# A four-layer graph network on one core: layer 0's hyperedge gather in two fp32r parts, the degrees' count in one pass, and a second buffer for each one-hot

## The chip, the cores and the metric

The kernel runs on one core of a Trainium2 chip. A core has a matrix engine (TensorE, PE in the profile, with its weight loads as PEld), three engines for elementwise work (VectorE as DVE, ScalarE as ACT, GpSimd as POOL), a queue engine that issues most transfers (SyncE, SP), and 16 DMA engines. Times are microseconds on the device for one execution. The kernel before was timed in three runs: 1318.43 us in the median, 1313.73 to 1319.35.

## The reference

Eight graphs share 2048 nodes of 64 features (x is 8 x 2048 x 64) and one adjacency of 2048 x 2048, whose rows are divided by their sums. Four layers follow each other, each as `x = layernorm(x + layer(x))`:

- Layer 0: `A_stack = [I, A, 2 A A - I]`, `x_g = A_stack x`, and for each node its own weights, `w = embedding weight`, 64 x 64 for each of the three terms, from 16 embedding numbers.
- Layer 1: a hypergraph attention. With `h = x W`, scores `s = leaky_relu(h a_node)` and the incidence `H` (2048 nodes by 64 hyperedges), `alpha` is the softmax of s over the nodes of a hyperedge, and

```
agg = jnp.einsum('ben,bnf->bef', alpha, h)
```

  gathers the nodes' features into every hyperedge. Gates, a second softmax over the hyperedges of a node, an average over the neighbours (`adj / deg`) and a mix of two sources come after it.
- Layer 2: `x Ws + A x Wn + bias`.
- Layer 3: a graph convolution with `A + I`, normalised on both sides by `1 / sqrt(deg)`.

## The kernel before

**Precision.** Two number formats reach TensorE. A plain fp32 matmul is shown in the trace as two records; one on tiles that were rounded to fp32r (`r_()` in the code is that view of the same bytes) as one. Large products are done in fp32r without loss that matters: the adjacency becomes a mask of zeros and ones, [...] and the other side is written as a high part (rounded) and a low part (the rest), `hi + lo`, with one matmul for each into the same accumulator. The row's scale is applied to the sum.

**Tiling.** Nodes are cut into 16 tiles of 128. A tile's features for all eight graphs are 128 x 512. A product with the adjacency is 16 tiles times 16 tiles times two parts, 512 matmuls of 128x128 by 128x512.

**The first product** (`first_product`, L422) computes A x, in 32 pieces of the adjacency. Between the pieces, `memberships` (L304) prepares the lists of hyperedges of the nodes, a step at a time, in four quarters of 512 nodes: from the transposed incidence (pT) come running counts (pf, one matmul), and VectorE compares them with 1 and 2 (oh01, L379) and with 3 and the overflow's positions (oh23, L382 and L415). The results, one-hots, are stored to DRAM by SP (`store`, L337); layer 1 loads them again. VectorE also makes the masks m that TensorE multiplies by (L458).

**Layer 0** (`layer0`, L954) follows the order in which its loop is written (`program_order` ties each engine to it). Pass j treats tile j in eight turns g. In each turn, `weigh` (L1094) multiplies three terms (x, y1, y2) by one part of the weights into pp (12 fp32 matmuls, 24 records), and VectorE adds four slices of pp, each scaled by a column of the embedding, to the residual r (L1115). Between the turns stands other work, for neighbouring tiles:

- g = 0 to 2: the layernorm of tile j - 1, in three steps. sq (L1128, ScalarE) is its square, var (L1132, VectorE) the reader of sq. The result x1 goes to DRAM (kept, L1159). The first terms of tile j + 1 are prepared.
- g = 3: `project(j - 2)` (L1185): h and the neighbour features of tile j - 2, then md (GpSimd, L1197), which is the incidence of the tile twice side by side, and hs (GpSimd, L1219), which is h times the exponential of the score. After it, on TensorE, the 32 matmuls of the second product for tile j + 1 (y2p, L1067), then `to_features(j - 1)` (L1161: trx on TensorE, xT on ScalarE). On GpSimd, `scaled` (L1005): ms, and the sums cs of the mask over its column blocks.
- g = 5: `compare` (VectorE, L1022) tests the adjacency against the mask.
- g = 6: `second_term(j + 1)`, `scores(j - 1)` (sgp, es), and `gather(j - 2)` (L1223): one fp32 matmul, aggp += md x hs.
- g = 7: `degrees(j + 1)` (L1086): one fp32 matmul of cs with a column of ones, into dgp.

In pass 16 there is no tile left to weigh: the layernorm of tile 15 ends, tiles 14 and 15 are projected, `spread` (L1226) makes md for all tiles again, denominators are summed, the last two gathers are made, and matmuls of layer 1's first neighbour product (ind, L1252) are put between. Layer 1 begins with agg, aggp times the reciprocal of the denominators (L549).

**Buffers.** Tiles of layer 0 live in sixteen areas b0_0 to b0_15 of 128 x 512 that are free until layer 1; `homes` (L965) says which tag uses which: hs has area 5, sq has area 15, cs has 13 and 14. Tags without a home come from the pool l0s; x1 has one buffer. A write to a buffer waits until the readers of what lay there before are done. oh01 and oh23 have one buffer each, so a quarter's comparison waits for the stores of the quarter before.

Of the kernel before, what the change touches and what calls it, by code (L numbers as in the profile page):

```python
# [8 lines left out]
F32 = mybir.dt.float32  # L9
# [3 lines left out]
ALU = mybir.AluOpType  # L13
# [5 lines left out]
P = 128  # L19
NT = N // P  # L20
# [37 lines left out]
def r_(ap):  # L58
    return ap.bitcast(F32R)
# [3 lines left out]
def kernel(  # L63
# [33 lines left out]
    make_identity(nc, ident)  # L97
    ident_r = const.tile([P, P], F32, tag="ident_r", name="ident_r")
    nc.vector.tensor_copy(r_(ident_r), ident)
    ones = const.tile([P, P], F32, tag="ones", name="ones")  # L100
    nc.vector.memset(ones, 1.0)
    eps_t = const.tile([P, 1], F32, tag="eps", name="eps_t")
    nc.vector.memset(eps_t, EPS)
    flag = const.tile([P, 1], mybir.dt.int32, tag="flag", name="flag")
# [15 lines left out]
    def b_view(t2):  # L120
        return t2.rearrange("p (b c) -> p b c", b=B)

    def bcast(small):
        return small.unsqueeze(2).to_broadcast([P, B, C])
# [179 lines left out]
    def memberships(pre, ps, pm, fcw_sb, fcb_sb, fcg_sb):  # L304
# [59 lines left out]
        for q in range(NQ):  # L364

            raw = raws.pop(q)
            pT = pre.tile([P, QW], F32, tag="pT", name=f"pT_{q}")
            nc.vector.tensor_scalar(r_(pT), raw, 0.0, None, op0=ALU.is_gt)
            nc.sync.dma_start(lists["pT"][q], pT[0:E])
            yield  # L370
            pf = ps.tile([P, QW], F32, tag="li", name=f"pf_{q}")
            nc.tensor.matmul(
                pf, r_(tri.rearrange("p h e -> p (h e)")), r_(pT[0:E]), start=True, stop=True
            )
            yield
            pfm = raw
            nc.vector.tensor_tensor(pfm, pf, pT, ALU.mult)
            oh01 = pre.tile([P, QW], F32, tag="oh01", name=f"oh01_{q}")
            nc.vector.tensor_scalar(r_(oh01), pfm, order01, None, op0=ALU.is_equal)  # L379
            store(q, oh01, 0)  # L380
            oh23 = pre.tile([P, QW], F32, tag="oh23", name=f"oh23_{q}")
            nc.vector.tensor_scalar(r_(oh23[0:64]), pfm[0:64], 3.0, None, op0=ALU.is_equal)  # L382
            if q + 1 < NQ:
                load(q + 1)
            S = pre.tile([P, 4, P], F32, tag="S", name=f"S_{q}")
            yield
            for t in range(4):

                j = 4 * q + t
                cols = slice(t * P, (t + 1) * P)  # L390
                sm = ps.tile([P, QW], F32, tag="li", name=f"sm_{j}")
                nc.tensor.matmul(
                    sm[:, 0:E], r_(pT[0:E, cols]), r_(tri[:, 0, :]), start=True, stop=True
                )
# [559 lines left out]
    def layer0(  # L954
# [7 lines left out]
        raws, msk, terms, resid, norm, srow = {}, {}, {}, {}, {}, {}  # L962
        x1s, xTs, hps, hss, mds = {}, {}, {}, {}, {}

        homes = {"xT": (0, 1, 2), "xs": (3, 4), "hs": (5,), "y1T": (6, 7), "r": (8, 9),  # L965
                 "y2": (10,), "y2T": (11, 12), "cs": (13, 14), "sq": (15,)}
        turn = {}

# [36 lines left out]
        def scaled(j, h):  # L1005

            m = msk[j, h]
            ms = tile("ms", f"ms_{j}_{h}", (P, 8, P))
            nc.gpsimd.tensor_tensor(  # L1009
                ms, m, srow[j].unsqueeze(1).to_broadcast([P, 8, P]), ALU.mult  # L1010
            )
            cs = tile("cs", f"cs_{j}_{h}", (P, 4, P))
            nc.gpsimd.tensor_tensor(cs, m[:, 0:4], m[:, 4:8], ALU.add)
            nc.gpsimd.tensor_tensor(cs[:, 0:2], cs[:, 0:2], cs[:, 2:4], ALU.add)
            nc.gpsimd.tensor_tensor(cs[:, 0], cs[:, 0], cs[:, 1], ALU.add)
            if h == 1:
                nc.gpsimd.tensor_tensor(cs[:, 0], cs[:, 0], msk[j, 0, "s"][1][:, 0], ALU.add)
            msk[j, h, "s"] = ms, cs

        def compare(j, h):  # L1020
            ms, cs = msk[j, h, "s"]
# [64 lines left out]
        def degrees(j):  # L1086

            dp = ps_tr.tile([P, QW], F32, tag="tr", name=f"dgp_{j}")
            nc.tensor.matmul(
                dp[:, 0:1], msk[j, 1, "s"][1][:, 0], ones[:, 0:1], start=True, stop=True  # L1090
            )
            nc.scalar.copy(deg[:, j:j + 1], dp[:, 0:1])

# [91 lines left out]
        def project(j, h_first=False):  # L1185
# [8 lines left out]
                    )  # L1194
            if j not in mds:
                md = tile("md", f"md_{j}", (P, 2, E))
                nc.gpsimd.tensor_copy(md, pm[:, j, :].unsqueeze(1).to_broadcast([P, 2, E]))  # L1197
                mds[j] = md.rearrange("p h e -> p (h e)")

            def by_half(t):  # L1200
# [14 lines left out]
            if not stay:  # L1215
                for t, kept_part in zip((hi, lo), kept_i[j]):
                    nc.sync.dma_start(kept_part, t)
            hss[j] = tile("hs", f"hs_{j}", bufs=1)
            nc.gpsimd.tensor_tensor(  # L1219
                b_view(hss[j]), b_view(h_sb[:, j, :]), bcast(es[:, j, :]), ALU.mult  # L1220
            )

        def gather(j):  # L1223
            nc.tensor.matmul(aggp, mds[j], hss[j], start=j == 0, stop=j == NT - 1)  # L1224

        def spread():  # L1226

            mds.clear()
            for q, home in enumerate((1, 2, 3, 10)):
                md = own.tile([P, 4, 2, E], F32, tag=f"b0_{home}", name=f"md4_{q}")  # L1230
                nc.gpsimd.tensor_copy(
                    md, pm[:, 4 * q:4 * q + 4].unsqueeze(2).to_broadcast([P, 4, 2, E])
                )
                for t in range(4):
                    mds[4 * q + t] = md[:, t].rearrange("p h e -> p (h e)")
# [39 lines left out]
        def when(j, f, *args):  # L1275
            if 0 <= j < NT:
                f(j, *args)
# [8 lines left out]
        with program_order():  # L1286
# [6 lines left out]
            for j in range(NT + 1):  # L1293
# [4 lines left out]
                for g in range(8):  # L1298
# [37 lines left out]
                        when(j + 2, mask, 1)  # L1336
                    elif g == 5:
                        when(j + 1, compare, 1)
                        if j:
                            next(flags, None)  # L1340
                    elif g == 6:
# [808 lines left out]
```

## Time and profile before

| what | us |
|---|---|
| profiled execution | 1318.67 |
| its span, first to last instruction | 1316.8 |
| median of three runs | 1318.43 |
| TensorE busy | 1259.5 |
| VectorE busy | 885.0 |
| GpSimd busy | 483.5 |
| ScalarE busy | 368.4 |
| first product, in the chain of work | 6.9 to 150 |
| layer 0, first y2p to last pp | 155 to 700 |
| one pass of layer 0 | 34.0 |
| aggp, 16 fp32 matmuls: median of one record | 0.634 |
| dgp, 16 fp32 matmuls: median of one record | 0.260 |

The mean granted TensorE clock was 0.973. A record's duration is not what it adds to the time: matmuls are pipelined, so 32 of them with 0.39 to 0.5 us each follow each other in 7.5 us. What one adds is read from the distance between starts, or from the chain of work, which is the path followed back from the last instruction, at every step to what released it.

### The profile page before, as it was taken

To read this page: it belongs to the slowest core of one execution; us is meant where nothing else is said; L and a number is where in the kernel's file an instruction comes from. 1 tells how busy PE (TensorE), PEld (TensorE's weight loads), DVE (VectorE), ACT (ScalarE), POOL (GpSimd) and SP (SyncE) were. 2 spreads that over 40 slices of the span, in tenths; PEclk is the share of its full clock that TensorE was granted. 3 is DMA by queue.
4 is the path that set the end of the run, shared out by engine and by line. 5 is a ranking of instruction groups with operands and counts; after the bars stand their busy time and mean duration, and the time that the engine had idled before them with its cause. 6 is when DMAs were issued, how large, how long until landed. Compare 5 with 4: busy or idle time off the path is not lost.

```text
span 1316.8 us, 19976 instructions
## 1 busy us (share of the span) xinstructions
PE 1259.5 (96%) x7708; PEld 1002.4 (76%) x7708; DVE 885.0 (67%) x1595; ACT 368.4 (28%) x837; POOL 483.5 (37%) x403
## 2 busy tenths in 40 slices
PE   7999799999999999999999699999998899999996
PEld 6777588888888888888887467777776788888885
DVE  5555268888777877888664568878874655565544
ACT  3000001221122222221222356666664621111111
POOL 1000264444444444444411468888873600000000
PEclk9999799999999999999998589999998999999998
DMA  9887733332333332222272212222220133234551
GB/s 294 238 222 136 215 100 101 107 98 100 107 107 107 106 102 94 94 94 102 81 240 67 103 71 98 96 96 97 81 96 0 50 144 115 109 128 147 176 185 70
DMA packets 100791, 157.22 MB, mean 119 GB/s; under 512 B 12880, under 2 KB 64464, under 8 KB 94672
## 3 DMA queue, kind: packets, MB, share of 16 engines
q1 hardware_dynamic: 98208, 151.65, 35.7%
q10 hardware_dynamic: 2304, 4.20, 0.8%
q8 instruction: 63, 1.03, 0.3%
q0 software_dynamic: 176, 0.02, 0.1%
q14 instruction: 40, 0.33, 0.1%
HBM read 118.08 MB, written 37.76 MB: 118 GB/s over the span
## 4 chain that ended last, share of the span: by engine, by line
PE 89%; DVE 3%; DMA 2%; issue 2%; ACT 2%; POOL 1%; SPq 0%; ACTq 0%; DVEq 0%; POOLq 0%
PE pp L1104 25%; PE a L1418 18%; PE y2p L1067 9%; PE ind L1418 9%; PE y1p L490 8%; PE fc L805 3%; PE df L814 2%; PE gp L705 1%; PE yp L1508 1%; PE try L165 1%; PE trm L165 1%; PE aggp L1224 1%; PE hp L1192 1%; PE sgp L1171 1%; PE red L746 1%
## 5 line engine op out<-in xcount | busy, mean ns | idle before, releaser
L1115 DVE SCALAR_TENSOR_TENSOR r<-pp,emb_sb,r 128x256 f32<-128x256 f32 x512 | 247.4, 483 | 114.8 <-PE pp L1104 100.6
L1104 PE MATMUL pp<-w_sb,xT 64*128 64x256 f32 x1024 | 160.4, 390 | 1.7 <-DVE r L1115 1.7
L1104 PE MATMUL pp<-w_sb,y1T 64*128 64x256 f32 x1024 | 153.5, 376 | 0.0
L1104 PE MATMUL pp<-w_sb,y2T 64*128 64x256 f32 x1024 | 153.5, 376 | 0.0
L1053 POOL TENSOR_TENSOR r<-xs,bn 128x256 f32<-128x256 f32 x32 | 22.7, 731 | 277.2 <-issue 245.4
L1104 PEld LDWEIGHTS pp<-w_sb,xT 64*128 64x128 f32 x1024 | 94.4, 186 | 25.1 <-issue 14.9
L490 PE MATMUL y1p<-x_hi,m 128*128 128x512 f32 x256 | 106.2, 415 | 6.9 <-ACT x_hi L436 6.9
L1104 PEld LDWEIGHTS pp<-w_sb,y1T 64*128 64x128 f32 x1024 | 99.7, 187 | 10.9
L1104 PEld LDWEIGHTS pp<-w_sb,y2T 64*128 64x128 f32 x1024 | 99.6, 187 | 11.0
L1067 PE MATMUL y2p<-y_hi,msk 128*128 128x512 f32 x256 | 103.5, 404 | 0.0
L490 PE MATMUL y1p<-x_lo,m 128*128 128x512 f32 x256 | 103.0, 402 | 0.0
L1418 PE MATMUL ind<-y_hi,mj_l 128*128 128x512 f32 x240 | 101.7, 424 | 0.0
L1067 PE MATMUL y2p<-y_lo,msk 128*128 128x512 f32 x256 | 101.5, 397 | 0.0
L1418 PE MATMUL a<-v_hi,mj_l 128*128 128x512 f32 x256 | 100.1, 392 | 0.0
L1418 PE MATMUL a<-v_lo,mj_l 128*128 128x512 f32 x256 | 99.9, 391 | 0.0
L1418 PE MATMUL a<-y_lo,mj_l 128*128 128x512 f32 x240 | 95.1, 396 | 0.0
L1418 PE MATMUL a<-y_hi,mj_l 128*128 128x512 f32 x240 | 94.9, 396 | 0.0
L1418 PE MATMUL ind<-y_lo,mj_l 128*128 128x512 f32 x240 | 94.6, 394 | 0.0
L1009 POOL TENSOR_TENSOR ms<-msk,srow 128x1024 f32<-128x1024 f32 x32 | 89.8, 2807 | 5.3 <-DVE ms L1022 5.3
L737 POOL TENSOR_TENSOR ez<-ez,coef 128x1024 f32<-128x1024 f32 x32 | 69.8, 2182 | 56.3 <-DVE ez L735 54.3
L1001 DVE TENSOR_SCALAR msk<-adj 128x1024 fp32r<-128x1024 f32 x32 | 63.7, 2024 | 9.2 <-DMA adj<-in_at 9.2
L490 PEld LDWEIGHTS y1p<-x_hi,m 128*128 128x128 f32 x256 | 49.6, 194 | 19.0 <-ACT x_hi L436 6.9
(279 smaller groups left out, 2391.8 us busy)
## 6 DMA issues: line engine op xcount, KB each, us to landing
mj_l<-mask SPq DMA_DIRECT2D x46, 1024.0 KB, 4.9
raw<-in_at SPq DMA_DIRECT2D x32, 512.0 KB, 5.1
adj<-in_at SPq DMA_DIRECT2D x64, 256.0 KB, 3.8
mask<-msk SPq DMA_DIRECT2D x32, 512.0 KB, 4.6
xraw<-in_xn SPq DMA_DIRECT2D x8, 512.0 KB, 4.6
oh<-oh SPq DMA_DIRECT2D x32, 128.0 KB, 2.8
xT<-in_xt SPq DMA_DIRECT2D x16, 256.0 KB, 3.0
xs<-in_xn SPq DMA_DIRECT2D x16, 256.0 KB, 2.9
```

The lines of the kernel that those rows point to most:

```text
L165: nc.tensor.matmul(dst, src, ident, start=True, stop=True, is_transpose=True)
L490: nc.tensor.matmul(accs[q][jj], r_(m[:, t, jj * P:(jj + 1) * P]), r_(part[:, mt, :]), start=i + h + t == 0 and part is x_hi, stop=i == 3 a ...
L737: nc.gpsimd.tensor_tensor(by_b(ez), by_b(ez), per_b(coef, 2 * i, 2), ALU.mult)
L805: nc.tensor.matmul(fc[:, h, :], fcw_sb[rs], sT[rs], start=True, stop=True)
L814: nc.tensor.matmul(df[:, b:b + 1], th[:, b % 2, (b // 2) * P:(b // 2 + 1) * P], av_sb, start=True, stop=True,)
L1001: nc.vector.tensor_scalar(r_(m), raws[j][h], 0.0, None, op0=ALU.is_gt)
L1009: nc.gpsimd.tensor_tensor(ms, m, srow[j].unsqueeze(1).to_broadcast([P, 8, P]), ALU.mult)
L1053: nc.gpsimd.tensor_tensor(r[:, 4 * bq * C:4 * (bq + 1) * C] .rearrange("p (h l c) -> p h l c", h=2, l=2), swapped(terms[j]["xs"], bq), bn. ...
L1067: nc.tensor.matmul(acc, r_(msk[j, mt // 8][:, mt % 8, :]), r_(part[:, mt, :]), start=mt == 0 and part is y_hi, stop=mt == NT - 1 and part ...
L1104: nc.tensor.matmul(pp[:, h, pl, :], terms[j][name][rs, 2 * bq + pl], w_sb[rs, k, dq * 4 * C:(dq + 1) * 4 * C], start=k == 0, stop=k == K - 1,)
L1115: nc.vector.scalar_tensor_tensor(rb, ppv[:, :, dd, :], emb_sb[:, j, d:d + 1], rb, op0=ALU.mult, op1=ALU.add)
L1418: nc.tensor.matmul(acc, r_(a[:, mt, :]), r_(part[:, mt, :]), start=mt == 0 and part is hi, stop=mt == NT - 1 and part is lo,)
```

## The change

- `gather` for tiles 0 to 14 uses a high and a low part of hs, two fp32r matmuls in place of one fp32 matmul. Tile 15 keeps the fp32 matmul. hs itself is now written to area 15 (tag hsf), with sq; ScalarE copies it to the high part, in area 5; GpSimd subtracts to get the low part, in the buffer of x1, at g = 5 (`low_part`). md is written with the fp32r view.
- `degrees`: the last of the sums of cs is written, with the fp32r view, to a tile of its own (both, one buffer), and multiplied by two columns of ones in fp32r (ones_r, written once at the start).
- oh01 and oh23 have two buffers each.

The edits of `homes`, `md` and the declaration of ones_r are left to these words; the rest is:

```diff
-            oh01 = pre.tile([P, QW], F32, tag="oh01", name=f"oh01_{q}")
+            oh01 = pre.tile([P, QW], F32, tag="oh01", name=f"oh01_{q}", bufs=2)
...
-            oh23 = pre.tile([P, QW], F32, tag="oh23", name=f"oh23_{q}")
+            oh23 = pre.tile([P, QW], F32, tag="oh23", name=f"oh23_{q}", bufs=2)
...
+            msk[j, h, "s"] = ms, cs
             if h == 1:
-                nc.gpsimd.tensor_tensor(cs[:, 0], cs[:, 0], msk[j, 0, "s"][1][:, 0], ALU.add)
-            msk[j, h, "s"] = ms, cs
+                both = tile("both", f"both_{j}", (P, P), 1)
+                nc.gpsimd.tensor_tensor(r_(both), cs[:, 0], msk[j, 0, "s"][1][:, 0], ALU.add)
+                msk[j, "sum"] = both
...
             nc.tensor.matmul(
-                dp[:, 0:1], msk[j, 1, "s"][1][:, 0], ones[:, 0:1], start=True, stop=True
+                dp[:, 0:2], r_(msk[j, "sum"]), r_(ones_r), start=True, stop=True
             )
...
-            hss[j] = tile("hs", f"hs_{j}", bufs=1)
+            hs = tile("hsf", f"hs_{j}")
             nc.gpsimd.tensor_tensor(
-                b_view(hss[j]), b_view(h_sb[:, j, :]), bcast(es[:, j, :]), ALU.mult
+                b_view(hs), b_view(h_sb[:, j, :]), bcast(es[:, j, :]), ALU.mult
             )
+            if j == NT - 1:
+                hss[j] = hs,
+                return
+            hss[j] = tile("hs", f"hs_hi_{j}"), hs
+            nc.scalar.copy(r_(hss[j][0]), hs)
+
+        def low_part(j):
+            if j < NT - 1:
+                hi, hs = hss[j]
+                lo = tile("x1", f"hs_lo_{j}", bufs=1)
+                nc.gpsimd.tensor_tensor(r_(lo), hs, hi, ALU.subtract)
+                hss[j] = hi, lo
 
         def gather(j):
-            nc.tensor.matmul(aggp, mds[j], hss[j], start=j == 0, stop=j == NT - 1)
+            for part in hss[j]:
+                a, b = (mds[j], part) if j == NT - 1 else (r_(mds[j]), r_(part))
+                nc.tensor.matmul(
+                    aggp, a, b, start=j == 0 and part is hss[0][0], stop=j == NT - 1
+                )
...
                     elif g == 5:
                         when(j + 1, compare, 1)
+                        when(j - 2, low_part)
```

More of the change, by code (lines that the diff above doesn't have):

```diff
@@ L99 @@
     nc.vector.tensor_copy(r_(ident_r), ident)
+    ones_r = const.tile([P, 2], F32, tag="ones_r", name="ones_r")
     ones = const.tile([P, P], F32, tag="ones", name="ones")
     nc.vector.memset(ones, 1.0)
+    nc.vector.tensor_copy(r_(ones_r), ones[:, 0:2])
     eps_t = const.tile([P, 1], F32, tag="eps", name="eps_t")
@@ L963, in layer0 @@
         x1s, xTs, hps, hss, mds = {}, {}, {}, {}, {}
-        homes = {"xT": (0, 1, 2), "xs": (3, 4), "hs": (5,), "y1T": (6, 7), "r": (8, 9),
+        homes = {"xT": (0, 1, 2), "xs": (3, 4), "hs": (5,), "hsf": (15,), "y1T": (6, 7), "r": (8, 9),
                  "y2": (10,), "y2T": (11, 12), "cs": (13, 14), "sq": (15,)}
@@ L1196, in project @@
                 md = tile("md", f"md_{j}", (P, 2, E))
-                nc.gpsimd.tensor_copy(md, pm[:, j, :].unsqueeze(1).to_broadcast([P, 2, E]))
+                nc.gpsimd.tensor_copy(r_(md), pm[:, j, :].unsqueeze(1).to_broadcast([P, 2, E]))
                 mds[j] = md.rearrange("p h e -> p (h e)")
@@ L1231, in spread @@
                 nc.gpsimd.tensor_copy(
-                    md, pm[:, 4 * q:4 * q + 4].unsqueeze(2).to_broadcast([P, 4, 2, E])
+                    r_(md), pm[:, 4 * q:4 * q + 4].unsqueeze(2).to_broadcast([P, 4, 2, E])
                 )
```

## The prediction

> **What bounds the kernel now.** I read the page's busy times first, then a table of stretches, then the chain of work of one stage of layer 0, then TensorE's waits there, and last the two places where the change could touch the order of things: the end of layer 0 and the end of the first product.
>
> ```profile
> PE 1259.5 (96%) x7708; PEld 1002.4 (76%) x7708; DVE 885.0 (67%) x1595; ACT 368.4 (28%) x837; POOL 483.5 (37%) x403
> ```
>
> TensorE is busy 96% of the span. Matmul ends are modelled, so this alone proves little; the stretch from 500 to 600 us, which is the middle of layer 0, says more (columns: length, then busy time and instruction count of PE, PEld, DVE, ACT, POOL, then granted clock, DMA share, GB/s):
>
> ```profile
> core 0: us, PE busy (x) PEld busy (x) DVE busy (x) ACT busy (x) POOL busy (x), PEclk, DMA share, GB/s
> 500.00:600.00 100.00, 100.00 (x787) 83.74 (x787) 78.48 (x141) 20.09 (x40) 46.97 (x42) 1.00 0.32 106
> ```
>
> TensorE has no gap, at full clock; VectorE is at 78%, ScalarE at 20%, GpSimd at 47%, DMA at a third. The chain of work from 448 to 482 us, one stage of layer 0 (start, length, engine and tile), is TensorE alone:
>
> ```profile
> 447.94 7.53 PE y2p L1067 x32
> 455.47 0.44 PE trx L165 x4
> 455.91 7.97 PE pp L1104 x72
> 463.88 0.59 PE try L165 x4
> 464.47 0.79 PE sgp L1171 x8
> 465.26 0.96 PE aggp L1224 x2
> 466.22 2.79 PE pp L1104 x24
> 469.01 0.31 PE dgp L1089 x2
> 469.32 7.97 PE pp L1104 x72
> 477.29 0.58 PE try L165 x4
> 477.88 0.36 PE bp L1048 x2
> 478.24 2.79 PE pp L1104 x24
> ```
>
> The gather (aggp) holds 0.96 us of a stage of 34 us, in two records: one fp32 matmul is recorded as two. The degrees' count (dgp) holds 0.31, also two. The product y2p is fp32r already: 32 matmuls of the same shape, 128x128 by 128x512, in 7.53 us, 0.235 each. What TensorE waits for from 176 to 690 us (us in total, times, longest) is almost nothing:
>
> ```profile
> PE pp L1104 <- DVE r L1115: 1.7, 3, 1.1
> PE sgp L1171 <- DVE flagbox L281: 0.2, 1, 0.2
> ```
>
> So in layer 0 a microsecond less on TensorE is a microsecond less of time, until something else is late.
>
> [...] 0.96 against 0.235 us for the same shape is 4.1. [...] this trace has 1.27 us for 128x512 (cs at 459.77), and I use that.
>
> **The gather.** Removed: 15 of 16 fp32 matmuls (the last tile keeps its own). Added: 30 fp32r matmuls. At y2p's spacing a pair is 2 x 0.235 = 0.47, so a gather saves 0.96 - 0.47 = 0.49. Fourteen (tiles 0 to 13) lie in TensorE-bound time: 14 x 0.49 = 6.9 us. No trace shows fp32r between an fp32 sgp and an fp32 pp. If both weight loads came as bare as those of sgp, whose records follow each other at 0.1 us (0.79 for 8), the pair would be 0.47 + 2 x 0.1, and the saving 0.3 a gather, 4.2 us; if the switch to fp32 that L1224 shows start to start (1.03 us from 465.12 to 466.15) went too, 0.56 and 7.8 us. I take 6.9, since y2p follows fp32 hp and precedes fp32 trx without a gap.
>
> Added beside it, per tile: a ScalarE copy of hs to its high part, 128x512, 0.59 us (as L1166), and a GpSimd subtraction for the low part, 1.27 us as above. In the steady stage both are covered. hs ends on GpSimd at 450.2; ScalarE is then idle until y2 at 455.57. The low part stands in GpSimd's queue behind the mask sums, which end at 457.5, and needs the x1 buffer, which trx leaves at 455.9 and the store issued at 446.98 has left before. It ends near 458.8; the gather comes at 465.1. Cover: 6.3 us; beyond it every stage pays the excess. What stands behind the low part on GpSimd (ms, cs, y1, r) has the slack of r's idle time before it, 17 us. The new homes add waits that are over early: hs now shares a buffer with sq, whose last reader ends at 444.1, five us before hs; the next sq is written at 475.6, 17 us after the low part. SP issues the same transfers in the same order through all this. The copies of pm that round to fp32r are the same copies (0.30 us), and one sum of cs goes to a new tile: nothing.
>
> **The degrees' count.** Sixteen fp32 matmuls with one column become fp32r with two; one record in place of two. Half of 0.31 is 0.155, so 16 x 0.155 = 2.5 us saved. Not shown: such a matmul between fp32 ones. The ends are 0 (the switch is all of its cost) and 3.2 (0.2 each). I take 2.4, for a little overhead.
>
> **The end of layer 0.** Here no TensorE work covers latency. The timeline (start, length):
>
> ```profile
> 710.98 0.59 ACT L1211 ACTIVATE h<-hp 128x512 f32<-128x512 f32 x1
> 711.46 0.59 ACT L1166 COPY xT<-trx 128x512 f32<-128x512 f32 x1
> 711.65 1.04 POOL L1219 TENSOR_TENSOR hs<-h,es 128x512 f32<-128x512 f32 x1 [4.33 <-ACT h L1211]
> 712.11 1.05 PE L1171 MATMUL sgp<-wa,xT 128*128 128x4 f32 x8 [1.08 <-ACT xT L1166]
> 715.67 1.04 POOL L1219 TENSOR_TENSOR hs<-h,es 128x512 f32<-128x512 f32 x1 [2.97 <-PE aggp L1224]
> ```
>
> The copy of tile 14's high part is put into ScalarE's queue between h and xT of tile 15, and it waits for hs, which ends at 712.69. So xT of 15 starts at about 713.3 and not 711.46: sgp, es, hp, h of 15 and all behind them are 1.8 us later. Given back: today hs of 15 waits for gather 14 (one buffer; last line), and will not; and gather 14 is 0.5 shorter. Walking it through: gather 14 starts at 716.3, six early matmuls of 0.235 end near 718.2, hs of 15 is ready at 717.9, so the last gather starts at 718.0 to 718.2 where it was 716.77. Cost 1.3 us; bounds 0.5 and 1.9. The same copy at tile 13 delays xT of 14 from 686.9 to 688.8, but sgp wants it at 695.5: nothing. SP moves one mask load behind the last kept and xr transfers; the list loads behind it start at 719.1, after layer 0 frees its memory, anyway: nothing.
>
> **Two buffers for each one-hot.** They take away a wait of VectorE for the stores of the quarter before. In the trace of before there is one place where that can have bound:
>
> ```profile
> 122.90 1.02 DVE L379 TENSOR_SCALAR oh<-pT_raw,order 128x512 fp32r<-128x512 f32 x1
> 123.84 0.40 DVE L382 TENSOR_SCALAR oh<-pT_raw 64x512 fp32r<-64x512 f32 x1
> ```
>
> The other three L379 take 0.49, and this L382 follows 0.54 late. At most 0.5 us, in the last quarter; the end of the first product then hangs on a transfer of the one-hots (123.95, 11.6 us in the chain), on SP behind it, and on adj's masks. I take 0, bounds -0.5 and 0. One more VectorE copy of 128x2 at the start is 0.2 us (as the other small ones) while the first transfers are awaited: nothing.
>
> **The sum.** The profiled execution took 1318.67 us (span 1316.8), 0.2 above the median of 1318.43. 1318.67 - 6.9 - 2.4 + 1.3 + 0 = 1310.7; against the median 1310.4. I say 1310.5.
>
> **Rivals.** (a) *Half of it.* The fp32r pair pays its weight loads and the degrees gain nothing: -4.2 - 0.6 + 1.5 = -3.3, some 1315. For it: L1224 and dgp sit between fp32 matmuls of 64 rows, and "issue" gaps of 0.3 us stand at such switches on the weight loads' row. Against it: y2p has none. (b) *VectorE becomes the bound* behind the shorter stretch: near 1317. For it: pp waits for r now and then (1.7 us). Against: 78% busy and 76 us of waits for pp from 210 to 650. (c) *Slower:* GpSimd's writes rounded to fp32r (md 0.30, both 0.45, low part 1.27, 2.02 in all) are slow, since this trace times no such large operation. TensorE then waits at the gather for the low part. With a factor f the low part is 2.02 x (f - 1) later, the cover of 6.3 is used up at f = 4.1, and the change loses from f = 4.5 on; at f = 5 it is 1.8 us in 14 stages, 25 us, so about 1336. Against: DVE and ACT rows with fp32r outputs take what f32 ones take.
>
> **How the numbers follow.** Forecast 0.65, (a) 0.22, (b) 0.05, (c) 0.05; 0.03 is for a larger gain, near 1306. A measurement of this kernel can tell about 0.5%, 6.6 us; the runs before spread from 1313.7 to 1319.4. The gains' own bounds give 1318.67 - 7.8 - 3.2 - 0.5 + 0.5 = 1307.7 and 1318.67 - 4.2 - 0 + 1.9 = 1316.4; with the spread of runs below, 1305.5 to 1316. Below 1311.8 lies most of the forecast and the larger gain: faster 0.66; (a), (b) and the forecast's upper part: same 0.29; slower 0.05.
>
> **What would show it.** Right: aggp about 0.47 in the chain of a stage, dgp under 0.2, a stage of about 33.35 in place of 34, TensorE without waits for the low part, xT of tile 15 behind the high part's copy by 1.8 us, agg 1.2 to 1.4 us later in relation to the last trx. Wrong: a wait of aggp for GpSimd; a pair above 0.7; the first product ending earlier or later by over a microsecond, since the work there moves on transfers that I do not price.

## The result, and the profile after

The kernel after took 1314.09 us in the median of 20 runs (1310.22 to 1316.33), the kernel before 1317.99 beside it (20 runs, 1313.11 to 1322.38): a ratio of 0.9972, with an interval of 0.9959 to 0.9986. That is 3.9 us saved where about 8 were forecast. The time lies inside the range that was given, 1305.5 to 1316.

Two more comparisons of the same two kernels, on two chips, gave 0.9981 (0.9967 to 0.9995) and 0.9954 (0.9938 to 0.9970). The third lies outside the interval of the first: executions of one kernel differ by more than the interval from one set of runs says, and what they differ in is the granted clock of TensorE (the kernel before took 1312.34 us at 0.979 and 1322.97 at 0.970). Much of what follows is about telling that apart from the change.

First the page of the kernel after, its row of busy times, against 1259.5, 885.0, 368.4 and 483.5 us before:

```profile
PE 1253.7 (95%) x7692; PEld 1002.0 (76%) x7692; DVE 886.6 (67%) x1596; ACT 377.9 (29%) x852; POOL 514.4 (39%) x418
```

TensorE has 5.8 us less, GpSimd 31 more (the low parts), ScalarE 9.5 more (the high parts). The table of stretches from 500 to 600 us (columns as in the prediction) says that the steady stage has kept its bound:

```profile
500.00:600.00 100.00, 100.00 (x795) 84.37 (x791) 79.74 (x144) 22.53 (x44) 53.65 (x45) 1.00 0.31 106
```

TensorE is still without a gap, at full clock, and does 795 records where it did 787. The waits of TensorE from 176 to 690 us (total, times, longest) are what they were, and none is for GpSimd:

```profile
PE pp L1109 <- DVE r L1120: 1.8, 3, 1.1
```

So the low part is hidden, and VectorE has not become the bound. The distance from one y2 copy on ScalarE to the next, which is one pass of layer 0, fell from 33.99 to 33.48 us; 33.35 had been forecast. Where the 0.51 came from is read from TensorE's timeline in one pass (start, length; `64*128` are the rows and columns of the array in use), start to start. Before:

```profile
465.12 1.10 PE L1224 MATMUL aggp<-hs,md 128*128 128x512 f32 x2
466.15 0.70 PE L1104 MATMUL pp<-w_sb,xT 64*128 64x256 f32 x4
...
468.94 0.38 PE L1089 MATMUL dgp<-ones,cs 128*128 128x1 f32 x2
469.25 0.70 PE L1104 MATMUL pp<-w_sb,xT 64*128 64x256 f32 x4
```

After:

```profile
462.35 0.48 PE L1245 MATMUL aggp<-hs_hi,md 128*128 128x512 f32 x1
462.66 0.40 PE L1245 MATMUL aggp<-hs_lo,md 128*128 128x512 f32 x1
462.99 0.70 PE L1109 MATMUL pp<-w_sb,xT 64*128 64x256 f32 x4
...
465.78 0.27 PE L1094 MATMUL dgp<-ones_r,both 128*128 128x2 f32 x1
465.98 0.70 PE L1109 MATMUL pp<-w_sb,xT 64*128 64x256 f32 x4
```

The gather holds TensorE for 462.99 - 462.35 = 0.64 us where it held it for 466.15 - 465.12 = 1.03: it saves 0.39 to 0.40, not 0.49. The two matmuls come 0.31 and 0.33 apart, not 0.235. The degrees' count holds 0.20 where it held 0.31: it saves 0.11, not 0.155. Both together are the 0.51.

The rest of the shortfall is at the end of layer 0. The chain of work of the kernel after there (start, length, engine and tile; `issue` is time in which no wait shows):

```profile
705.08 1.05 POOL hs L1224
706.13 0.02 issue
706.15 0.02 ACT hs_hi L1231
706.17 0.50 issue
706.68 0.59 ACT xT L1171
707.26 0.04 issue
707.31 1.87 PE sgp L1176 x8
709.17 2.01 PE hp L1197 x16
711.18 0.52 PE denp L1262 x2
711.71 1.05 PE aggp L1245 x2
712.76 1.59 PE ind L1275 x6
714.35 0.86 PE aggp L1245 x2
```

The copy of tile 14's high part stands in front of xT of tile 15 and waits for hs. From trx of tile 15 to its sgp there were 1.74 us before (710.37 to 712.11); now there are 3.58 (703.73 to 707.31), 1.84 more, the very number that was forecast. But sgp then takes 1.87 us where it took 1.05, and hp 2.01 where it took 1.09: behind the hole TensorE works at half clock (a granted clock of 0.50 from 707.31 to 711.18). From the start of trx to the start of agg it is 11.52 us where it was 7.56, which is 3.96 more against the 1.3 of the forecast.

### The profile page after: what moved, and what is told of

It reads as the page before. It is cut to its first block, busy times and chain, and to the rows that moved or that the text cites. A ratio compares the mean times of both kernels' runs of the same rounds, so it can differ in the third digit from the quotient of the medians.

```text
span 1314.5 us, 19978 instructions
## 1 busy us (share of the span) xinstructions
PE 1253.7 (95%) x7692; PEld 1002.0 (76%) x7692; DVE 886.6 (67%) x1596; ACT 377.9 (29%) x852; POOL 514.4 (39%) x418
## 3 DMA queue, kind: packets, MB, share of 16 engines
q8 instruction: 63, 1.03, 0.3%
```

## The experiments

Two readings are used throughout. *Fourteen passes* is the time from the first y2 copy to the fifteenth; it is the same within 0.05 us in every profile of a kernel. Layer 0 is still filling in the first of these passes, so the fourteen hold 11 gathers and 14 counts of degrees. The *mean clock* is the granted clock of TensorE over a whole run, which every run lists. Within one kernel the time goes with it: of 56 runs of the kernel before on one chip, the 16 at 0.970 took 1322.07 in the median, the 16 at 0.973 took 1318.26, and the 10 at 0.978 took 1313.14. Over all runs of all kernels here, a thousandth of mean clock is 0.99 us, by the slope within the kernels. The last but one column of the table moves each kernel's mean to a clock of 0.973 with that slope (with twice its standard error), so that kernels can be compared whose runs happened to get different clocks. It also takes out a loss of clock that the kernel may itself have caused; that is why the medians stand beside it. It differs by 0.6 us between chips for the kernel before (1318.2 to 1318.8), and it is weakest for the kernel with the lowest clock, high part of 14 later, which it moves by 3.4 us.

| kernel | runs | median us | mean clock | mean us, moved to 0.973 | fourteen passes |
|---|---|---|---|---|---|
| before (all but the first comparison's) | 156 | 1318.21 | 0.9736 | 1318.5 ± 0.1 | 460.54 |
| after (all) | 53 | 1314.05 | 0.9716 | 1312.3 ± 0.3 | 454.66 |
| two buffers alone | 14 | 1320.28 | 0.9722 | 1318.8 ± 0.5 | 460.54 |
| degrees alone | 22 | 1316.82 | 0.9731 | 1316.1 ± 0.5 | 459.05 |
| gather alone | 11 | 1312.31 | 0.9736 | 1313.4 ± 0.5 | 456.08 |
| high part of 14 later | 9 | 1313.53 | 0.9696 | 1309.7 ± 0.8 | 454.64 |
| gather 14 in fp32 | 16 | 1311.62 | 0.9732 | 1311.6 ± 0.4 | 454.66 |
| hole filled | 16 | 1313.30 | 0.9708 | 1310.6 ± 0.4 | 454.66 |
| gathers beside y2p | 22 | 1313.32 | 0.9725 | 1313.1 ± 0.5 | 454.68 |
| all three moves | 14 | 1309.61 | 0.9727 | 1309.7 ± 0.4 | 452.5 |

**The parts one by one.** The two buffers alone, on the kernel before:

```diff
-            oh01 = pre.tile([P, QW], F32, tag="oh01", name=f"oh01_{q}")
+            oh01 = pre.tile([P, QW], F32, tag="oh01", name=f"oh01_{q}", bufs=2)
...
-            oh23 = pre.tile([P, QW], F32, tag="oh23", name=f"oh23_{q}")
+            oh23 = pre.tile([P, QW], F32, tag="oh23", name=f"oh23_{q}", bufs=2)
```

> The kernel before with two buffers for each one-hot and nothing else. Two readings are used for all runs: the length of a pass of layer 0 (distance of two copies of y2 on ScalarE, 33.99 us before, 33.48 after) and the end of layer 0, from the start of the last trx of layer 0 to the start of agg (7.56 us before, 11.52 after). Theory (the one-hots never waited for a store that mattered): pass 33.99, end 7.6, the first L379 of the last quarter still 1.02 us, time within 0.2% of before. Rival (the 0.5 us by which the first y2 came later after the change is the price of the buffers): the first y2 again 0.5 us later than 165.0, time 0.5 us longer.

Measured: 1.0009 (0.9995 to 1.0022), passes as before to the hundredth, and 7.55 us from trx to agg. The buffers give nothing. The slow comparison that the prediction had pointed to is still there in the kernel after; VectorE's timeline:

```profile
123.55 1.02 DVE L381 TENSOR_SCALAR oh<-pT_raw,order 128x512 fp32r<-128x512 f32 x1
```

It takes 1.02 us with two buffers as with one, so the store of the quarter before was not what it waited for. What slowed it is not shown; beside it GpSimd issues a transfer in each of these traces (L473, 1.17 us from 123.17 here).

The degrees alone (the declaration of ones_r, the sum in `scaled` and the matmul in `degrees`, as in the change):

```diff
-                dp[:, 0:1], msk[j, 1, "s"][1][:, 0], ones[:, 0:1], start=True, stop=True
+                dp[:, 0:2], r_(msk[j, "sum"]), r_(ones_r), start=True, stop=True
```

> The kernel before with the degrees' count in fp32r alone. Theory (a count goes from 0.31 to 0.20 us, not to half): pass 33.88, end of layer 0 7.6 us, time 1.7 us shorter. Rival (the halving that was forecast): pass 33.84 or less, 2.5 us shorter.

Measured: 0.9983 (0.9972 to 0.9994), a pass of 33.88: 0.11 saved. Fourteen passes save 1.49. From trx to agg it is 10.61, though, where 7.6 was expected: this kernel has 10.24 us of half clock at the end of layer 0.

The gather alone (homes, md, hs with its parts, `low_part`, `gather`, as in the change):

```diff
+            hss[j] = tile("hs", f"hs_hi_{j}"), hs
+            nc.scalar.copy(r_(hss[j][0]), hs)
...
+                nc.gpsimd.tensor_tensor(r_(lo), hs, hi, ALU.subtract)
...
+                a, b = (mds[j], part) if j == NT - 1 else (r_(mds[j]), r_(part))
```

> The kernel before with the gather's two parts alone. Theory (the pair takes 0.64 us start to start where fp32 took 1.03, and the end of layer 0 loses 4 us through the copy of the high part and the clock that falls while TensorE waits for it): pass 33.59, end 11.5 us, time 1.5 to 2 us shorter. Rival (the end lost its time to something in the other two edits): pass 33.59, end under 9 us, time 4 us or more shorter.

Measured: 0.9957 (0.9943 to 0.9971), a pass of 33.59: 0.40 saved. Fourteen passes save 4.46, which with the degrees' 1.49 is 5.95; the kernel after saves 5.88 (11 x 0.40 + 14 x 0.11 = 5.9). The parts add up. The wait for xT is there with the gather alone (3.58 from trx to sgp), and not with the degrees alone (1.74). To agg it is 11.51, as expected; but the time is 6.4 us below the kernel before on the same chip and not 1.5 to 2, and 5.1 at equal clock.

**The late xT.** The copy of tile 14's high part is moved behind xT of tile 15 on ScalarE:

```diff
-            nc.scalar.copy(r_(hss[j][0]), hs)
+            if j < NT - 2:
+                nc.scalar.copy(r_(hss[j][0]), hs)
...
             if j < NT - 1:
                 hi, hs = hss[j]
+                if j == NT - 2:
+                    nc.scalar.copy(r_(hi), hs)
```

> The kernel after, with the high part's copy of tile 14 moved behind the copy of xT of tile 15 on ScalarE, nothing else. Theory (that copy's place is the whole cause of the loss at the end of layer 0: 1.84 us by itself, 2 more by the clock in the hole it makes): last trx to agg 7.0 to 7.6 us, granted clock 1.0 in sgp, hp and gather, pass 33.48, time 4 us shorter than after and 6 to 7 shorter than before. Rival (the end loses to the shared areas or to GpSimd's low part): end 10 us or more.

Measured: 0.9961 (0.9946 to 0.9976), 5.2 us below the kernel before where 6 to 7 were expected. From trx to sgp it is 1.74 again, so the copy's place was the cause of the hole. But it is still 10.45 from trx to agg, and not 7.0 to 7.6. The timeline of this kernel there, its GpSimd line and the VectorE line beside it:

```profile
704.18 1.27 POOL L1241 TENSOR_TENSOR hs_lo<-hs,hs_hi 128x512 fp32r<-128x512 f32 x1 [0.73 <-ACT sg L1181]
704.20 1.27 DVE L1184 SCALAR_TENSOR_TENSOR es<-sg 128x8 f32<-128x8 f32 x1 [1.21 <-ACT sg L1181]
```

VectorE's es takes 0.17 us elsewhere (703.05 in the third profile of the kernel after); here it takes 1.27, started 0.02 after GpSimd's low part and ended 0.02 after it. That the one held up the other is read from these two lengths; no run tests it alone. So this move ended one wait, and es took 1.1 us more. Only 0.37 of it reach TensorE, in which denp waits for es (hp, at half clock, ends at 705.60). The rest of the 10.45 goes with half clock: 13.66 us of it stand between 693.86 and 710.93.

The kernel after once more, as a measure on the same chip as the next three:

> The kernel after once more, unchanged. Passes of 33.48 us and xT of tile 15 behind the high part's copy again, sgp 3.5 us after the last trx starts. Theory A (the fall of the clock to half at the end of layer 0 comes from the hole of 2.9 us before sgp, every time): sgp, hp and the gathers again at half clock, last trx to agg 11.5 us. Theory B (the clock is halved in blocks of 3.4 us whose place differs from execution to execution): the half-clock blocks lie elsewhere in relation to the last trx, and trx to agg is anything between 9.0 (full clock: 7.56 plus 1.84 less what the shorter gather and the second buffer give back) and 12 us.

Measured: 0.9981 (0.9967 to 0.9995), 1314.88. The profile is like the first: 3.58 from trx to sgp, sgp 1.87, 11.62 from trx to agg.

The gather of tile 14 in fp32 as before, without parts, so that nothing stands in front of xT:

```diff
-            if j == NT - 1:
+            if j >= NT - 2:
                 hss[j] = hs,
                 return
...
-            if j < NT - 1:
+            if j < NT - 2:
                 hi, hs = hss[j]
...
-                a, b = (mds[j], part) if j == NT - 1 else (r_(mds[j]), r_(part))
+                a, b = (mds[j], part) if j >= NT - 2 else (r_(mds[j]), r_(part))
```

> The kernel after, with the gather of tile 14 in fp32 as that of tile 15, so that no copy and no low part lie at the end of layer 0. Passes 33.48 us. Theory (the end loses 1.84 us by the late xT, and its hole makes half clock likelier): sgp 1.7 us after the last trx starts, time 2 to 4 us shorter than after again. Rival (the end is decided by the clock alone and the place of the copy hardly counts): within 1 us of after again.

Measured: 0.9950 (0.9931 to 0.9968), 1311.62, which is 3.3 below the kernel after on the same chip. From trx to sgp it is 1.74. Yet its profile also has 13.66 us of half clock and 10.65 from trx to agg, and of the 3.3 some 2.5 go with a better mean clock (0.9732 against 0.9708). What the hole itself costs is nearer to the 0.7 of the table than to the 3.3 of the medians: from the first y2 to agg, with 13.66 us of half clock in each, it is 548.8 here and 549.7 in the first profile of the kernel after.

**The switch.** Each gather is put behind hp and in front of y2p, which are already at such an edge (`gather(j - 3)` behind `project(j - 2)`):

```diff
                     elif g == 3:
                         when(j - 2, project)
+                        when(j - 3, gather)
...
                         when(j - 1, scores)
-                        if j < NT:
-                            when(j - 2, gather)
-                        else:
+                        if j == NT:
```

> The kernel after, with each gather one pass turn later, between hp and the 32 matmuls of y2p. Theory (a pair takes 0.64 us because its first matmul and the fp32 one behind it each come 0.1 us late at a change of format or of row group, as y2p's first does with 0.34): beside y2p it adds 0.46 and not 0.64, pass 33.30, 2.5 us shorter than after again. Rival (fp32r with these operands is slower by itself): the pair again 0.64 apart, pass 33.48.

Measured: 0.9971 (0.9958 to 0.9984), 1.6 us below the kernel after on the same chip where 2.5 were expected. TensorE's timeline in one pass:

```profile
474.83 1.06 PE L1197 MATMUL hp<-wb,xT 64*128 64x128 f32 x16
475.82 0.50 PE L1245 MATMUL aggp<-hs_hi,md 128*128 128x512 f32 x1
476.16 0.39 PE L1245 MATMUL aggp<-hs_lo,md 128*128 128x512 f32 x1
476.39 0.39 PE L1072 MATMUL y2p<-y_hi,msk 128*128 128x512 f32 x1
```

The first of a row of fp32r matmuls takes 0.34, every further one 0.23, and that first one comes once, whether it is aggp's or y2p's. A steady pass is 33.36, 0.12 less than after: 0.19 is saved at the gather, and 0.07 comes back at sgp, whose last matmul now stands in front of pp (the eight hold TensorE for 0.88, where it was 0.81). So the pair's surplus, some 0.1 us on each side of the gather, goes with its neighbours and not with its operands.

What stands at such an edge is seen in the weight loads (PEld). Before, at the start of a row of y2p, at its end, and at the gather:

```profile
447.87 0.19 PEld L1067 LDWEIGHTS y2p<-y_hi,msk 128*128 128x128 f32 x1
447.98 0.19 PEld L1067 LDWEIGHTS y2p<-y_lo,msk 128*128 128x128 f32 x1
448.21 0.19 PEld L1067 LDWEIGHTS y2p<-y_hi,msk 128*128 128x128 f32 x1
...
455.08 0.37 PEld L165 LDWEIGHTS trx<-ident,x 128*128 128x128 f32 x2
...
465.09 0.30 PEld L1224 LDWEIGHTS aggp<-hs,md 128*128 128x128 f32 x2
466.15 0.19 PEld L1104 LDWEIGHTS pp<-w_sb,xT 64*128 64x128 f32 x2 [0.76 <-issue]
```

After, at the gather:

```profile
462.32 0.19 PEld L1245 LDWEIGHTS aggp<-hs_hi,md 128*128 128x128 f32 x1
462.43 0.19 PEld L1245 LDWEIGHTS aggp<-hs_lo,md 128*128 128x128 f32 x1
462.99 0.19 PEld L1109 LDWEIGHTS pp<-w_sb,xT 64*128 64x128 f32 x2 [0.36 <-issue]
```

Within a row a load starts with the matmul in front of its own, 0.23 us early (448.21 for the matmul at 448.44). At an edge it starts with its own matmul (447.87; 462.99 and 466.15 for pp) or 0.03 early (462.32 for 462.35, 465.09 for 465.12). So the edges belong to both formats, and the fp32 gather paid them too: where its neighbours had 128 rows, in the kernel after at tile 15 (the last line of the chain above), it held TensorE for 0.86 us, and between sgp and pp for 1.03. The fp32 transposes trx (128 rows) follow the fp32r row without an edge, at 0.23 (455.08 to 455.31); pp (64 rows) does not. That the late load makes the edge is read from this order; no run tests it alone.

Over fourteen passes nothing of it is left (454.68 against 454.66): an early pass takes 34.24 where it took 33.56, and TensorE waits 2.8 us for VectorE's r where it waited 1.8; the rest of that loss is not found.

The three moves together: tile 14 in fp32, the gathers beside y2p, and the degrees' count at g = 6 ahead of the transposes of y:

```diff
                     elif g == 6:
+                        when(j + 1, degrees)
                         when(j + 1, second_term)
...
-                    elif g == 7:
-                        when(j + 1, degrees)
```

> e5_plain14 with the gather beside y2p and the degrees' count moved from behind the seventh to behind the sixth turn's weighing, ahead of the transposes try. Theory (the count pays 0.1 us for a change that it then shares with try): pass 33.20, and 5 us shorter than after again, 8 to 9 shorter than before. Rival: pass 33.30, since the count costs its 0.20 wherever it stands.

Measured: 0.9941 (0.9921 to 0.9962), 1310.92, which is 4.0 below the kernel after and 6.7 below the kernel before on the same chip, less than expected; but a steady pass of 33.09, less than either theory had. The count now stands between pp and the transposes, where an edge is paid anyway:

```profile
459.11 0.27 PE L1094 MATMUL dgp<-ones_r,both 128*128 128x2 f32 x1
459.24 0.66 PE L167 MATMUL try<-ident,y 128*128 128x128 f32 x4
```

It holds TensorE for 0.13 in place of 0.20, and the pp that it had cut in two, 2.79 and 7.97 us, take 10.56 in one piece. Together that is 0.27 a pass; the count's 0.20 had left out the edges in pp. The fifth to the eighth pass gain nothing. By its median this is the fastest version of all, ahead of both kernels.

**The clock.** Two theories for the half clock at the end of layer 0 were tested: A, that the hole in TensorE's work causes it; B, that it falls differently in every execution. Each kernel once more, for one profile:

> The kernel before once more, for a second profile of its end of layer 0. Theory A (a hole in TensorE's work is what halves the granted clock there, so that kernels without the late xT are spared): trx to agg 7.5 to 7.6 again, sgp of tile 15 at 1.05, full clock behind trx of tile 15. Theory B (where the clock is halved differs from one execution to the next, whatever the kernel): 7.5 to 10.7, and the half-clock stretches stand elsewhere than at 702.8 to 709.9; the span then goes with the mean clock of the execution, about 1.04 us for each 0.001: 1316.8 at 0.973, 1320 at 0.970, 1311 at 0.979. Both: 33.99 a pass.

> A third profile of the kernel before, with the same expectations as the second: A 7.5 to 7.6 from trx to agg again; B anything from 7.5 to 10.7, and a span that goes with the mean clock.

> A third profile of the kernel after. A: trx to agg 11.5 to 11.6 and sgp of tile 15 at 1.87, as in the first two. B: the wait for xT is 2.9 again, but the clock behind it may be full, and trx to agg then 9.2 to 9.5 (7.56 + 1.84, the six matmuls of ind not counted). Both: 33.48 a pass, 3.58 from trx to sgp.

Measured: the second profile of the kernel before has a span of 1312.5 at 0.978, no half clock at the end of layer 0 and 7.33 from trx to agg; the third has 1316.1 at 0.973 and 7.56. The third of the kernel after took 1309.35, with sgp at 1.05, 2.97 from trx to sgp (trx itself waits 0.53 for x here) and 9.84 to agg. The table of stretches, from 690 to 717 us, in the first profile of before, the second of before, the first of after and the third of after (the third number from the right is the granted clock):

```profile
690.00:717.00 27.00, 25.92 (x182) 21.41 (x179) 12.98 (x30) 5.45 (x13) 4.16 (x4) 0.87 0.10 30
```

```profile
690.00:717.00 27.00, 25.15 (x186) 19.98 (x182) 14.24 (x37) 6.29 (x14) 3.77 (x3) 1.00 0.15 42
```

```profile
690.00:717.00 27.00, 24.08 (x136) 19.75 (x135) 9.69 (x27) 6.47 (x15) 5.04 (x4) 0.75 0.11 36
```

```profile
690.00:717.00 27.00, 22.97 (x149) 17.55 (x146) 10.48 (x26) 6.77 (x13) 5.02 (x4) 0.94 0.32 103
```

The same kernel has 0.87 and 1.00, or 0.75 and 0.94. Read at finer steps, the stretches of half clock at the end of layer 0 are 3.41 or 6.83 us long in every profile, and longer elsewhere (27.31 us at 0.50, from 740.13 to 767.44, in the first profile of before): whole multiples of one length, but for the last, which ends with the kernel. Executions of one kernel have them at different places: between 690 and 717 us they start at 702.58 in the first profile of before, at 701.79 in the third and nowhere in the second; in the four of after at 696.03 and 706.27, at 695.26 and 705.50, at 703.63, and at 694.31 and 704.55. What sets the length and the starts was not shown. A as it was stated falls with the third profile of the kernel after, where sgp took 1.05 behind a hole; B stands for how much half clock an execution gets. The 3.58 from trx to sgp that both expected was missed, and so were B's 9.2 to 9.5 to agg. From trx to agg, though, the kernel before stayed at 7.33 to 7.56, as A had it: in its profiles half clock fell ahead of trx or not at all, and B's 10.7 was not seen. Whether a hole makes half clock likelier is a weaker claim. On the grid of 3.41 us that the starts and lengths in one profile make, half clock did follow that hole, one step later; the third profile of the kernel after:

```profile
700.22:703.63 3.41, 1.87 (x22) 1.85 (x24) 0.34 (x2) 1.51 (x5) 1.62 (x2) 1.00 0.12 44
703.63:707.04 3.41, 3.41 (x14) 2.71 (x11) 0.97 (x3) 1.12 (x3) 1.04 (x1) 0.50 0.00 0
```

In all eight profiles of kernels in which TensorE waits 2.2 to 2.9 us around this trx (the kernel after four times, the gather alone, the gathers beside y2p, and the two shifted ones below), the step that holds most of the wait is followed by half clock. Where it waits 1.1 to 1.4 us, that is so in six profiles of ten: not in the three of the kernel before and not with two buffers alone, but with the degrees alone, which has no late xT either. So a long wait was always followed by half clock here, and a short one often. Whether that makes the mean clock lower, the next kernel bears on. Six matmuls of ind, which until then stood behind gather 14, are put into the hole:

```diff
                         when(j - 1, to_features)
+                        if j == NT:
+                            early[0](3)
...
-            early[0](3)
             gather(NT - 1)
```

> The kernel after with six matmuls of layer 1's first neighbour product, which stood between the two last gathers, put behind trx of tile 15, so that TensorE works during 1.4 us of the wait for xT. trx to sgp stays 3.58 in both theories. A (the hole halves the clock): sgp of tile 15 takes 1.05 and not 1.87, trx to agg falls from 11.5 to 7.8 to 8.5 (1.4 moved, and some 2 of half clock gone), and the time is 2 to 3 below the kernel after, 1311 to 1312. B (the clock does not depend on it): trx to agg 10.1 (11.5 less the 1.4 moved) when halved, 8 when not, and the time 1.0 to 1.4 below the kernel after, near 1313.

Measured: 0.9965 (0.9948 to 0.9981), 1313.30; from trx to sgp it is 3.00, as in the third profile of after and not 3.58; TensorE waits 0.84 us for xT, sgp takes 1.05, but half clock runs from 703.22 to 710.05 and it is 11.11 to agg. Theory A's 7.8 to 8.5 is missed, and the mean clock over 16 runs, 0.9708, is no better than the kernel after's. B's 10.1 is missed too, by 1.0. At equal clock the time is 1.7 below the kernel after, near what B expects of the matmuls moved.

Last, kernels that only move the moment at which layer 0 ends. The count of tile 15 is made seven or fifteen times over:

```diff
-            nc.tensor.matmul(
-                dp[:, 0:2], r_(msk[j, "sum"]), r_(ones_r), start=True, stop=True
-            )
+            for _ in range(15 if j == NT - 1 else 1):
+                nc.tensor.matmul(
+                    dp[:, 0:2], r_(msk[j, "sum"]), r_(ones_r), start=True, stop=True
+                )
```

> The kernel after again, as the measure for the two shifted ones: 1314.0 to 1314.9 in the median, mean clock over its runs 0.9705 to 0.972.

> The kernel after with the degrees' count of tile 15 made seven times over (the same result each time), which moves the end of layer 0 by six times 0.13, some 0.8 us, and nothing else. Theory H (the hole lowers the clock, wherever it falls): mean clock as in the kernel after, within 0.0007, and 0.8 us more. Theory P (the clock is set window by window, some 3.4 us each, and what counts is where the sparse stretches fall in the windows): the mean clock over the runs moves by 0.001 or more, up or down, and the time by 1 us or more against the 0.8 that was added.

> The same with fifteen counts in place of one, a shift of fourteen times 0.13, some 1.8 us, about half of a stretch of half clock. H: mean clock as in the kernel after, and 1.8 us more. P: the mean clock moves by 0.001 or more; if the windows run from the program's start, this shift should show the most, up to 0.003, and the time could then even be below the kernel after.

> The fastest version again (tile 14's gather in fp32, the other gathers beside y2p, the counts ahead of the transposes of y), for more runs: 1309.5 to 1311.5 in the median, ratio to before 0.993 to 0.996.

Measured: the kernel after 1311.78 (0.9954), mean clock 0.9728; six counts more 1313.51 (0.9961, 0.9949 to 0.9973), 0.9725; fourteen more 1312.04 (0.9950, 0.9931 to 0.9969), 0.9738; the three moves 1308.61 (0.9927, 0.9893 to 0.9960), 0.9740. In the profile of the larger shift the counts hold TensorE for 1.76 us (665.81 to 667.57) where one holds it for 0.20. The kernel after missed its own expectation by 2 us and more, at a better clock than in its other comparisons, and the three moves theirs by 0.9, downwards too. Against this kernel after, the small shift leaves the clock alone, as H expects, and the large one lifts it by 0.0010, the least that P asks; their times move by 1.7 and 0.3 us where H has 0.8 and 1.8. With 20 and 10 runs beside 10 of the kernel after, and 0.9708, 0.9718 and 0.9728 for one and the same kernel in three comparisons, this decides nothing between H and P. That the clock is set in windows was the author's supposition; the traces show the lengths, 3.41 us and its multiples.

## Why the prediction was wrong, by its steps

**What bounds the kernel, and what is hidden: right.** TensorE kept its 100% in the steady stage; no wait for the low part came up; VectorE at 79.7% is no bound. Rivals (b) and (c) did not come. (The rows with fp32r outputs that spoke against (c), in the trace of before, for 128x512: ScalarE 0.60 us for y_hi in fp32r and 0.59 for h in f32, both from hp; VectorE 0.68 for y_lo in fp32r at L880 and 0.68 for y2T in f32.) GpSimd's low part, written rounded to fp32r, took 1.27 us (704.18 above), as estimated.

**The gather: of the terms in the sum, the one that failed most.** "I take 6.9, since y2p follows fp32 hp and precedes fp32 trx without a gap." The second half is so, but trx has 128 rows and pp, which stands behind the gather, 64: the one follows the last fp32r matmul at 0.23, the other at 0.33. The first half was a misreading: 0.235 is 7.53 us divided by 32, and the mean hides the first of the row, which comes 0.34 apart (447.87 to 448.21 in the profile before, then 448.44). A row of 32 pays the edge once, a pair pays it once too, on 2 matmuls. So 0.47 was the price of a pair without edges, which takes 0.64 in its place; and the 0.96 set against it, read from the chain, was short of the 1.03 that the fp32 gather held TensorE start to start. Measured, a gather saves 1.03 - 0.64, some 0.40, where 0.49 was taken: 14 x 0.40 = 5.6 and not 6.9. It lies between the two ends that the prediction had named, 0.3 and 0.56; it had priced each of the two corrections, and took neither.

**The degrees: right in kind, too large.** 0.11 each and not 0.155: 16 x 0.11 = 1.8 and not 2.4. Two records became one, but the count still holds TensorE for 0.20, not for 0.155. "For a little overhead" had taken off 0.1 in all, where 0.7 was due.

**The two buffers: right.** Nothing, and the slow L379 did not wait for a store.

**The end of layer 0: the wait right, its cost right only at equal clock.** Where half clock lay ahead of trx, sgp came 1.84 us later, for the reason given and to the hundredth (in the chain above ScalarE begins hs_hi at 706.15 and xT behind it at 706.68; that it would keep this order was the author's estimate); with full clock there (the second profile of before, the third of after) it was 1.5 later, 2.97 behind trx and not 1.50. The first profile shows 3.96 us, not 1.3. To compare at an equal share of half clock, take the executions that have about 6.83 us of it between 690 and 717: before, twice, 552.94 us from the first y2 to agg; after, in its fourth profile, 547.07. That is 5.9 saved. With 3.41 us of it, the two buffers alone have 551.37 and the kernel after, in its third profile, 545.45: 5.9 again. The passes give 5.6 + 1.8 = 7.4, and so the end costs about 1.5, near the forecast.

**What the sum left out: the clock.** With the sizes measured the sum is -5.6 - 1.8 + 1.5 = -5.9, and the column at equal clock says 1312.33 - 1318.46 = -6.1 (on the two chips by themselves -6.3 and -6.4). The medians differ by 4.2, in the first comparison by 3.9; the mean clock was 0.9716 against 0.9736, and 2.0 thousandths are 2.0 us. So of the 4.1 us between the forecast's 8.0 and the 3.9, the gather accounts for 1.3, the degrees for 0.6, the end for 0.2, and the clock, a term that the sum put at nothing, for about 2. The prediction worked with one profile, in which the clock behind trx of tile 15 was full, and read the spread of the runs as noise without asking what it was made of.

Whether the change costs clock, or these runs had less of it, stays open. For it: over the pooled runs the difference is several times its standard error (0.0002 and 0.0003); half clock at the end of layer 0 was 13.65, 13.65, 3.41 and 6.82 us in the four profiles of after, and 6.83, none and 6.83 in the three of before (elsewhere in the run 63 to 64, and 60 to 67); and it followed the late xT every time. Against the hole as its cause: the kernel with gather 14 in fp32 has no hole and 13.66, the one with the degrees alone none and 10.24; the one with the hole filled has the mean clock of the kernel after; the gather alone has the hole and 0.9736. And against any firm answer: the same kernel got 0.9708 in one comparison and 0.9728 in another, beside 0.9742 and 0.9732 for the kernel before.

Rival (a), "half of it", forecast -3.3 and is near in number; its mechanism is half true. The edges are real and cost 0.1 us each. But it had put the degrees' gain at 0.6, and it did not have the clock, which is about half of what is missing in the medians.

## What to carry to other kernels

Price a short burst of matmuls from the first record of a row, start to start, not from the mean of a long row, and what it replaces in the same way; and put a small matmul where an edge is paid anyway (the degrees' count, moved so, gained 2.1 us over fourteen passes). Before a change of half a per cent is judged, lay the times of the runs beside their granted clocks: here one kernel spread over 10 us with its clock, and intervals from the runs of one comparison were too narrow. When an operation is moved off a queue, ask who will run beside it in its new place: with the high part moved out of xT's way, VectorE's es took 1.27 us beside GpSimd's low part, 1.1 more than elsewhere, of which 0.37 reached TensorE.

## What had not been expected of the hardware

- The granted clock at the end of layer 0 falls to half in stretches of 3.41 or 6.83 us, which start elsewhere in each execution (in the three profiles of the kernel before at 702.58, nowhere, and at 701.79). A wait of 2.2 to 2.9 us of TensorE there was followed by one in eight profiles of eight. With the mean clock, runs of the kernel before went from 1312.34 to 1322.97 us (156 runs, correlation -0.96).
- An edge between two kinds of matmul cost about 0.1 us, in fp32 and in fp32r: 0.31 to 0.34 in place of 0.23 for the first fp32r matmul of 128x512 behind sgp or hp; 0.33 from the last one to pp with 64 rows, but 0.23 to trx with 128; and 1.03 in place of 0.86 for an fp32 gather between sgp and pp. At these edges, where it was read, the weight load started with its own matmul or 0.03 before it; within a row of y2p it started 0.23 before.
- A VectorE operation of 0.17 us (es) took 1.27, once, beside a GpSimd operation of 1.27 (the low part).
